# A graph-attention layer on one Trainium2 core: a branch mark for TensorE, a separate bank for a quarter of an accumulator, and a reordered last stage without GpSimd

## The chip, the core and the metric

The kernel runs on one core of one Trainium2 chip. The core has five engines with an instruction queue each: TensorE (PE in the profile, with its weight loads as PEld), VectorE (DVE), ScalarE (ACT), GpSimd (POOL) and SyncE (SP), which issues most DMA transfers. Sixteen DMA engines serve all DMA queues of the core. Results of matmuls go to PSUM, which this kernel uses as eight banks of 128 partitions by 512 float32.

The metric is the device time of one execution in microseconds. The profile's span is shorter than that time, since it reaches only from the program's first to its last instruction.

## The reference

Two graph-attention layers, a residual and a layer norm, on 512 nodes of width 768. The edge list has 16,896 entries sorted by destination (8192 pairs in both directions and one loop per node).

```python
def gat_layer(x, W, a_s, a_d, b, edge_index, concat):
    h = (x @ W).reshape(n, H, C)
    alpha_s = jnp.einsum('nhc,hc->nh', h, a_s)
    alpha_d = jnp.einsum('nhc,hc->nh', h, a_d)
    e = jax.nn.leaky_relu(alpha_s[src] + alpha_d[dst], NEG_SLOPE)
    m = jax.ops.segment_max(e, dst, num_segments=n)
    e = jnp.exp(e - m[dst])
    denom = jax.ops.segment_sum(e, dst, num_segments=n)
    alpha = e / (denom[dst] + EPS)
    msg = h[src] * alpha[:, :, None]
    out = jax.ops.segment_sum(msg, dst, num_segments=n)
    return out.reshape(n, H * C) + b

h = jax.nn.elu(gat_layer(x, W1, a_src1, a_dst1, b1, edge_index, True))   # 8 heads of 768
out = gat_layer(h, W2, a_src2, a_dst2, b2, edge_index, True)             # 1 head of 768
return _layernorm(x + out, axis=-1)
```

## The kernel before, in words

The edge list is turned once into a dense 512 x 512 table of edge counts, so attention becomes dense matrix work. For each of the eight heads the kernel projects x, computes the logits, takes the masked softmax, multiplies the attention matrix with the projected features, applies elu and multiplies by that head's rows of W2, adding into `h2`. All products are made by fast matrix-multiplication schemes: seven products of half-size blocks P1 to P7 instead of eight, or fifteen of thirds, with sums of blocks on the vector engine before and after.

The order of instructions is written by hand. Strings such as `HEAD`, `SECOND`, `NEXT` and `END` list short names, and `run` calls the function behind each name in that order; each engine's queue is in the order in which its instructions were so emitted. The framework adds the semaphore waits. `mm` is a list of free PSUM banks: `mm.next()` takes the one that was freed longest ago, `mm.release` puts one back. A bank taken out and written by one engine is guarded as a whole against the others.

The **branch.** The first pass assumes a balanced edge list. It computes a flag, and after it `tc.If(again != 0, label="again")` (line 33) runs a general pass if the assumption failed. With these inputs it does not fail, so each engine's branch jumps over the whole general pass to the few closing instructions. `mark_branch_hint_location` marks that branch as likely taken for the engines it lists: ScalarE, VectorE and SyncE before the change.

The **last stage** (`END`, from `root` on) multiplies the attention matrix of layer 2 with `h2` by seven products for two row halves i = 0 and 1 (`final`, line 1348), which gives the four row tiles of the output: tiles 0 and 1 in the upper half, 2 and 3 in the lower. Three accumulators of 384 columns are used for each i:

- `A`, i: P1 and P2, the left half of tile i (`residual`, names `sA`, adds the residual x + b2 scaled by the softmax denominator).
- `B`, i: a copy of A after P1 (`fork`), then P6, P7 and P4: the left half of tile 2 + i. After P6 and after P7 the vector engine reads it (`zu`, `zw`).
- `F`, i: starts from the residual (`seed`), then P5. `y22` (line 1400 or 1402) reads it for the right half of tile 2 + i, which goes to the output buffer `y`. `sF` (`less_first`, line 1387) adds another residual in place, and P3 completes the right half of tile i. For i = 1, P3 is made in two column quarters `f.P3.1a` and `f.P3.1b` (`final_part`, line 1371).

The softmax denominator is not divided out; the layer norm's epsilon is scaled instead. For each tile t follow statistics of its halves (`bn`, lines 1412 and 1415), their aggregate and the square root on ScalarE (`all`, lines 1433 and 1435), the reciprocal and the offset on VectorE (`inv`, lines 1440 and 1442), and the scaling with the store: `whole` for tiles 0, 2 and 3 (line 1450 on GpSimd for the right half of tile 3, line 1448 on ScalarE for the rest; one store of 384 KB by SyncE, line 1462), `left1` and `right1` for tile 1, the last (VectorE with SyncE's store, ScalarE with its own store, 192 KB each, line 1455). After the branch, SyncE waits for every store's semaphore (line 33), and the launch's closing barrier (line 1514) ends the program.

Of the kernel before, what the change touches and what calls it, by code (L numbers as in the profile page):

```python
# [13 lines left out]
AF = mybir.ActivationFunctionType  # L14
ALU = mybir.AluOpType
# [22 lines left out]
def gat_pass(  # L38
# [29 lines left out]
    L, R = slice(0, HALF), slice(HALF, D)  # L68
# [38 lines left out]
    mm, held = Ring(banks[:3]), Ring(banks[3:])  # L107
# [197 lines left out]
    general = flag is None  # L305
# [10 lines left out]
    else:  # L316
# [5 lines left out]
        for c in range(EC):  # L322
            m = (c + 0.5) * P * N / E
# [34 lines left out]
        for j in range(2):  # L358
            for r in range(2):
# [10 lines left out]
                                op0=ALU.mult, op1=ALU.add)  # L370
# [45 lines left out]
    HS, AL, BC = {}, {}, {}  # L416
# [307 lines left out]
    def run(script, ops):  # L724
        for name in script.split():
            ops.pop(name)()

    def softmax(q, h):
        ops = {}

        def token(t):
            def up():
                q[t] = lift(h, t)

            def out():
# [27 lines left out]
    again = None  # L763
    if not general:
# [72 lines left out]
        ops = {f"hot{j}": f for j, f in enumerate(f for q_ in range(NT) for f in one_hots(q_))}  # L837
# [15 lines left out]
    else:  # L853
        for t in range(NT):
            ps = mm.next()
            for c in range(EC):
# [3 lines left out]
                                        op0=ALU.is_equal)  # L860
# [245 lines left out]
    ops = softmax(q, 0)  # L1106
# [13 lines left out]
    mm = Free([banks[(mm.at + 1 + j) % 3] for j in range(3)] + banks[3:])  # L1120
# [18 lines left out]
    def hold():  # L1139
# [25 lines left out]
        P61 P70 u1 w0 x0 w.P6 P71 P40 b0 vadd ls2 P30 w.P10 q.P1 q.P4 q.P7 y0 ld1 w1 B0 P51 P62 P41 u2 x1 w.P2 b1 P72 w2 ls3  # L1165
        ld2 P31 P42 f0 y1 B1 P52 f1 F0 m.P2 x2 b2 F1 g.P9 P32 B2 g.P12 y2 m.P9 e.P2 f2 m.P12 ld3 F2 g.P7 rows0 e.P9 g.P1 w.P3
        rows1 row2 e.P12 g.P13 m.P1 g.P6 g.P11 spread e.P1 m.P0 own m.P13 2lift1 2lift2 2lift0 2leak1 g.P10 e.P0 2rank1 e.P13
        2lift3 2leak0 2rank0 m.P10 m.P4 2part1 e.P10 2leak2 2part0 g.P8 m.P11 e.P4 2rank2 2leak3 m.P6 seed g.P3 m.P8 g.P14
        e.P6 2den0 2den2 2part2 2in1 m.P14 2rank3 e.P11 e.P8 g.P5 e.P14 2den3 2part3 m.P3 2in2 m.P7 2in0 2den1 e.P3 m.P5 e.P7
        2in3 root c0 a0 f.P1.0 f.P1.1 e.P5 seed0 seed1 f.fork0 a1 c1 f.P5.0 sA0 f.P6.0 a2 c2 f.P2.0 zu0  # L1170
        f.fork1 f.P7.0 a3 c3 f.P6.1 zw0 f.P4.0 y22.0 sq2 sF0 f.P3.0 zu1 bn2L sA1 all2 f.P7.1 bn0L bn0R inv2 whole2 all0 f.P5.1
        zw1 f.P4.1 inv0 whole0 y22.1 sF1 f.P2.1 bn3R bn3L all3 f.P3.1a bn1L inv3 f.P3.1b whole3 bn1Ra bn1Rb all1 hint inv1 left1
        right1"""
    NEXT = ["""t.P11 e.P3.1 T.P6 t.P1 M.P8 T.P2 t.P13 E.P8 T.P4 M.P13 E.P13 in1 M.P9 l0 E.P9 l1 in2 M.P2 E.P2 M.P4 T.P10 T.P0 E.P4
        in3 M.P12 E.P12 l2 T.P1 M.P6 r0 M.P0 E.P6 E.P0 M.P1 r1 E.P1 M.P10 r2 E.P10 M.P5 r3 E.P5 M.P14 T.P7 E.P14 l3 M.P11
        T.P3 E.P11 src2 M.P7 M.P3 E.P7 E.P3 dst3 dst2 src3""",
# [16 lines left out]
    for h in range(H - 1):  # L1193
        last = h + 2 == H
        ops = mixed(h, AA, BB)
# [44 lines left out]
        else:  # L1240
            G, gsums = g_thirds()
# [4 lines left out]
        if h == 0 and not general:  # L1246
            again = nc.values_load(flag[:1, :1], min_val=0, max_val=E)
# [19 lines left out]
    xr = load_x()  # L1267
# [59 lines left out]
    ops.update({f"2den{t}": dens_(t) for t in range(NT)})  # L1327
# [12 lines left out]
    bank, stats, mv, rstd, off = {}, {}, {}, {}, {}  # L1340
# [18 lines left out]
    def seed_(i):  # L1359
        def f():  # L1360
            bank["F", i] = mm.next()
            nc.scalar.activation(bank["F", i][:, :HALF], xr[:, 2 + i, L], AF.Copy, scale=whole_den[2 + i])
        return f

    Q = HALF // 2
    quarters = (slice(0, Q), slice(Q, HALF))

    def final_part(j):
        def f():
            for k in range(2):  # L1370
                nc.tensor.matmul(bank["F", 1][:, quarters[j]], A2["P3"][:, k, P:2 * P], C2["P3"][:, k, quarters[j]],
                                 start=False, stop=k == 1, skip_group_check=True)
        return f

    def part(name, i):
        return bank[name, i][:, :HALF]
# [6 lines left out]
        return lambda: nc.vector.scalar_tensor_tensor(part("A", i), xr[:, i, L], whole_den[i], part("A", i), op0=ALU.mult,  # L1383
                                                      op1=ALU.add)

    def less_first(i):
        return lambda: nc.vector.tensor_tensor(part("F", i), part("F", i), xr[:, i, R], op=ALU.add)
# [4 lines left out]
    y = [None]  # L1392

    def lower_right(i):
        def f():
            if y[0] is None:
                y[0] = hpool.tile([P, NT, D], F32, name="hs")
            o = y[0][:, 2 + i, R]
            if i:
                nc.vector.tensor_tensor(o, part("F", i), xr[:, 2 + i, R], op=ALU.add)  # L1400
            else:
                nc.vector.scalar_tensor_tensor(o, part("F", i), 1.0, xr[:, 2 + i, R], op0=ALU.mult, op1=ALU.add,
                                               accum_out=total)
        return f

    def half_of(t, cols):
        if cols == R:
            return part("F", t) if t < 2 else y[0][:, t, R]
        return part("A", t) if t < 2 else part("B", t - 2)

    def moments(t, cols):
        return lambda: nc.vector.bn_stats(stats[t][:, 0 if cols == L else 1, :], half_of(t, cols))

    def moments_part(j):
        return lambda: nc.vector.bn_stats(stats[1][:, 1 + j, :], part("F", 1)[:, quarters[j]])

    def spread_of(t):

# [23 lines left out]
            nc.vector.scalar_tensor_tensor(off[t], mv[t][:, 0:1], -1.0, rstd[t], op0=ALU.mult, op1=ALU.mult)  # L1442
        return f

    def scale(t, cols, engine):
        o = y[0][:, t, cols]
        if engine == nc.scalar:
            nc.scalar.activation(o, half_of(t, cols), AF.Identity, bias=off[t], scale=rstd[t])
        else:
            engine.tensor_scalar(o, half_of(t, cols), mv[t][:, 0:1], rstd[t], op0=ALU.subtract, op1=ALU.mult)  # L1450

    def row_out_half(cols, engine, queue):
        def f():
            scale(1, cols, engine)
            queue.dma_start(out[P:2 * P, cols], y[0][:, 1, cols])
        return f

    def row_out_whole(t):
        def f():
            scale(t, L, nc.scalar)  # L1460
            scale(t, R, nc.gpsimd if t == 3 else nc.scalar)
            nc.sync.dma_start(out[t * P:(t + 1) * P, :], y[0][:, t, :])
        return f

    for i in range(2):
        for p, name in (("P1", "A"), ("P2", "A"), ("P6", "B"), ("P7", "B"), ("P4", "B"), ("P5", "F"), ("P3", "F")):
            if (p, i) != ("P3", 1):
                ops[f"f.{p}.{i}"] = final(p, i, name)
        ops.update({f"f.fork{i}": fork_(i), f"zu{i}": less_(i, i), f"zw{i}": less_(i, 2 + i), f"sA{i}": residual(i),
                    f"seed{i}": seed_(i), f"sF{i}": less_first(i), f"y22.{i}": lower_right(i)})  # L1470
# [11 lines left out]
    ops.update(left1=row_out_half(L, nc.vector, nc.sync), right1=row_out_half(R, nc.scalar, nc.scalar))  # L1482

    def hint():
        if not general:
            tc.mark_branch_hint_location("again", "LikelyTaken", [mybir.EngineType.Activation, mybir.EngineType.DVE, mybir.EngineType.SP])
    ops["hint"] = hint
    run(END, ops)
    return again

# [28 lines left out]
```

## Time and profile before

| what | value |
|---|---|
| time, median of 3 runs (lowest to highest) | 612.53 us (611.76 to 612.70) |
| the profiled execution's own time | 611.53 us |
| its span, first to last instruction | 609.7 us |
| granted TensorE clock, mean | 0.997 |
| TensorE matmuls, busy | 600.4 us (98% of the span) |
| VectorE, busy | 517.9 us (85%) |
| ScalarE, busy | 305.4 us (50%) |
| GpSimd, busy | 100.6 us (17%) |

Busy time counts arithmetic and weight loads, not waits, branches, semaphores or the issuing of DMA transfers; these stand in the trace under the engine's name with a q behind it. A timeline row gives start and length in microseconds, engine, source line, operation, written tile, read tiles, shape and count, and in brackets how long the engine had been idle and what released it. `hs`, `mm`, `tr`, `bc`, `st` are the program's names of tiles: `mm`, `tr` and `bc` are the PSUM banks, `hs` is here the residual or the output buffer.

### The profile page before, as it was taken

The numbers are of one execution on the slowest core, as the hardware profiler recorded it, in microseconds if no ns is written. First come the engines' busy times: TensorE is split into PE (matmuls) and PEld (weight loads), VectorE is DVE, ScalarE is ACT, GpSimd is POOL, SyncE is SP. The second block draws the span as 40 slices with busy tenths as digits, with TensorE's granted clock in tenths as the row PEclk, the third lists the DMA queues.
The fourth block names the chain that finished last, engine by engine and source line by source line (L and its number), as shares of the span: only waits on it lengthen the run. The fifth ranks groups of instructions, "written<-read, shape, count | busy, mean of one in ns | idle before, by whom it ended". The sixth has DMA issues, their size and how long they took to land.

```text
span 609.7 us, 8353 instructions
## 1 busy us (share of the span) xinstructions
PE 600.4 (98%) x2812; PEld 492.3 (81%) x2812; DVE 517.9 (85%) x1027; ACT 305.4 (50%) x563; POOL 100.6 (17%) x140
## 2 busy tenths in 40 slices
PE   9999999999999999999999999999999999999994
PEld 5665685788888888888888888888888888887863
DVE  7979968779997789878897789977897789989984
ACT  3128776624745166442746066532755147744743
POOL 2210103040301302022300303012210304022001
PEclk9999999999999999999999999999999999999998
DMA  8973898794947959395955939297883949593203
GB/s 302 314 169 90 251 273 200 217 287 78 346 70 237 212 179 244 51 336 81 330 110 174 268 127 291 47 300 133 273 167 113 294 92 261 104 238 56 53 17 109
DMA packets 97343, 114.24 MB, mean 187 GB/s; under 512 B 42966, under 2 KB 78222, under 8 KB 96398
## 3 DMA queue, kind: packets, MB, share of 16 engines
q1 hardware_dynamic: 75230, 89.26, 45.9%
q0 software_dynamic: 21632, 23.79, 24.6%
q10 hardware_dynamic: 432, 0.59, 0.3%
q8 instruction: 24, 0.39, 0.3%
q14 instruction: 25, 0.20, 0.1%
HBM read 99.05 MB, written 2.90 MB: 167 GB/s over the span
## 4 chain that ended last, share of the span: by engine, by line
PE 98%; DVE 0%; ACT 0%; issue 0%; DVEq 0%
PE mm L552 22%; PE mm L472 18%; PE mm L986 17%; PE mm L413 12%; PE tr L552 5%; PE bc L986 4%; PE tr L472 4%; PE bc L472 4%; PE tr L986 3%; PE bc L552 3%; PE mm L1348 2%; PE mm L663 1%; PE bc L792 1%; PE tr L413 1%; PE bc L271 1%; PE bc L1348 0%
## 5 line engine op out<-in xcount | busy, mean ns | idle before, releaser
L560 DVE TENSOR_TENSOR h<-h,mm 128x512 f32<-128x512 f32 x74 | 50.5, 683 | 8.9 <-PE mm L552 8.1
L478 ACT ACTIVATE hs<-mm 128x512 f32<-128x512 f32 x26 | 15.5, 597 | 80.6 <-PE mm L472 79.9
L187 POOL DMA_DIRECT2D w2t<-in_L_gnn_W_dram x21 | 28.3, 1662 | 165.9 <-PE mm L472 84.0
L480 DVE TENSOR_TENSOR hs<-hs,mm 128x512 f32<-128x512 f32 x38 | 26.1, 687 | 27.0 <-PE mm L472 19.9
L986 PE MATMUL mm<-PT,hs 128*128 128x256 f32 x192 | 46.6, 380 | 0.0
L552 PE MATMUL mm<-w1r,gT 128*128 128x256 f32 x192 | 44.2, 380 | 0.0
L915 ACT ACTIVATE q<-q,rden 128x512 f32<-128x512 f32 x28 | 20.2, 720 | 42.7 <-DVE rden L899 42.5
L923 ACT COPY PT<-zr 128x1024 uint16<-128x1024 uint16 x35 | 40.4, 1158 | 2.2 <-DMA zr<-pS 1.2
L187 POOL DMA_DIRECT2D w2r<-in_L_gnn_W_dram x14 | 18.3, 1310 | 139.4 <-DVE gT L1038 77.3
L552 PEld LDWEIGHTS mm<-w1r,gT 128*128 128x128 f32 x192 | 36.4, 190 | 5.2 <-DVE gT L589 0.3
L986 PEld LDWEIGHTS mm<-PT,hs 128*128 128x128 f32 x192 | 36.2, 190 | 5.2 <-ACT u L997 0.2
L703 ACT ACTIVATE q<-q,nmax 128x512 f32<-128x512 f32 x36 | 26.0, 722 | 25.9 <-DVE nmax L700 25.9
L472 PE MATMUL mm<-w2r,gT 128*128 128x256 f32 x144 | 33.7, 379 | 0.0
L422 DVE SCALAR_TENSOR_TENSOR scr<-hs,a_s 128x768 bf16<-128x768 f32 x32 | 30.6, 955 | 0.7
L422 DVE SCALAR_TENSOR_TENSOR scr<-hs,a_d 128x768 bf16<-128x768 f32 x32 | 30.5, 952 | 0.3
L472 PEld LDWEIGHTS mm<-w2r,gT 128*128 128x128 f32 x144 | 27.3, 190 | 3.8 <-issue 0.2
L552 PE MATMUL mm<-w1t,gS 128*128 128x256 f32 x128 | 30.2, 379 | 0.0
L472 PE MATMUL mm<-w2r,xT 128*128 128x256 f32 x128 | 29.9, 379 | 0.0
L986 PE MATMUL mm<-pS,gS 128*128 128x256 f32 x120 | 29.3, 379 | 0.0
L918 ACT COPY pS<-q 128x1024 uint16<-128x1024 uint16 x27 | 28.1, 1045 | 0.7
L472 PEld LDWEIGHTS mm<-w2r,xT 128*128 128x128 f32 x128 | 24.3, 190 | 3.3
L552 PEld LDWEIGHTS mm<-w1t,gS 128*128 128x128 f32 x128 | 24.3, 190 | 3.3
(393 smaller groups left out, 1493.2 us busy)
## 6 DMA issues: line engine op xcount, KB each, us to landing
w2r<-in_L_gnn_W_dram SPq DMA_DIRECT2D x48, 384.0 KB
w1r<-in_L_gnn_W_dram SPq DMA_DIRECT2D x43, 384.0 KB
gT<-xd SPq DMA_DIRECT2D x6, 1280.0 KB
w2t<-in_L_gnn_W_dram SPq DMA_DIRECT2D x21, 256.0 KB
w2t<-in_L_gnn_W_dram POOLq DMA_DIRECT2D x21, 256.0 KB, 9.3
w1t<-in_L_gnn_W_dram SPq DMA_DIRECT2D x18, 256.0 KB
w1t<-in_L_gnn_W_dram POOLq DMA_DIRECT2D x18, 256.0 KB, 5.1
w2r<-in_L_gnn_W_dram POOLq DMA_DIRECT2D x14, 256.0 KB, 8.7
```

Of the source, the lines that this page charges most:

```text
L187: return lambda: nc.gpsimd.dma_start(o, part(k, n), accum_op=add)
L413: nc.tensor.matmul(ps[:, :HALF], A_[p][:, k, i * P:(i + 1) * P], B_[p][:, k, :], start=start and k == 0, stop=k == HK - 1, skip_group_chec ...
L422: return [lambda al=al, a=a, sign=sign: nc.vector.scalar_tensor_tensor(scr, HS[h][:, t, :], sign, a, op0=ALU.mult, op1=ALU.mult, accum_out ...
L472: nc.tensor.matmul(bank[chain][:, i * TH:(i + 1) * TH], A_[p][:, k, i * P:(i + 1) * P], B_[p][:, k, :], start=first and i == k == 0, stop= ...
L480: nc.vector.tensor_tensor(out(o), out(o), ps, op=how)
L552: nc.tensor.matmul(bank[chain][:, i * TH:(i + 1) * TH], A_[p][:, k, i * P:(i + 1) * P], B_[p][:, k, :], start=first and i == k == 0, stop= ...
L560: nc.vector.tensor_tensor(out(o), out(o), ps, op=how)
L703: nc.scalar.activation(q, q, AF.Exp, bias=nmax, scale=-1.0, accum_out=dens[t])
L915: nc.scalar.activation(q, q, AF.Copy, scale=rden)
L918: nc.scalar.copy(apart.rearrange("p (h n) -> p h n", h=2), q.bitcast(U16).rearrange("p (n h) -> p h n", h=2))
L923: copy(PT.rearrange("p s n -> p (s n)").bitcast(U16).rearrange("p (s n h) -> p s n h", s=NT, h=2)[:, :, t * P:(t + 1) * P, :], parted.pop( ...
L986: nc.tensor.matmul(st[bank][:, :HN], A_[p][:, k, c * P:(c + 1) * P], B_[p][:, k, :], start=start and k == 0, stop=k == 1, skip_group_check ...
```

## The change

Four edits, all in the last stage or for it.

1. `hintT` in `END`: the branch is marked as likely taken for TensorE too.
2. The bank that held the broadcast logits row of layer 2 (`BC[H]`) is put back into the list of free banks once its last reader has been emitted (`freed`). From it, indirectly, comes one more bank `G`: the add `sF1` is split in two column quarters, `sF1a` writes its sum to `G`, `sF1b` works in place in F, 1. `f.P3.1a`, its statistics `bn1Ra` and its scaling use `G`. The scaling of tile 1's right half becomes two instructions of 192 columns on ScalarE, followed by one store as before.
3. Both halves of tile 3 are scaled by ScalarE; GpSimd has no instruction left in the last stage.
4. The order: `y22.1` stands ahead of `inv0`, and the right statistics, left statistics and aggregate of tile 3 (`bn3R bn3L all3`) stand ahead of `sF1a`, with `inv3` and `whole3` between `sF1a` and `sF1b`. The order of the matmuls is the same.

```diff
-        2lift3 2leak0 2rank0 ...
+        2lift3 freed 2leak0 2rank0 ...
...
-        f.fork1 f.P7.0 a3 c3 f.P6.1 zw0 f.P4.0 y22.0 sq2 sF0 f.P3.0 zu1 bn2L sA1 all2 f.P7.1 bn0L bn0R inv2 whole2 all0 f.P5.1
-        zw1 f.P4.1 inv0 whole0 y22.1 sF1 f.P2.1 bn3R bn3L all3 f.P3.1a bn1L inv3 f.P3.1b whole3 bn1Ra bn1Rb all1 hint inv1 left1
-        right1"""
+        f.fork1 f.P7.0 a3 c3 f.P6.1 zw0 f.P4.0 y22.0 sq2 sF0 f.P3.0 zu1 bn2L sA1 all2 hintT f.P7.1 bn0L bn0R inv2 whole2 all0 f.P5.1
+        zw1 f.P4.1 y22.1 inv0 whole0 bn3R bn3L all3 f.P2.1 sF1a inv3 whole3 sF1b f.P3.1a f.P3.1b bn1L bn1Ra bn1Rb all1 hint inv1
+        left1 right1"""
...
+    ops.update(..., freed=lambda: mm.release(BC[H]))
...
     def final_part(j):
...
-                nc.tensor.matmul(bank["F", 1][:, quarters[j]], A2["P3"][:, k, P:2 * P], C2["P3"][:, k, quarters[j]],
+                nc.tensor.matmul(bank[("F", 1) if j else "G"][:, quarters[j]], A2["P3"][:, k, P:2 * P], C2["P3"][:, k, quarters[j]],
...
-    def less_first(i):
-        return lambda: nc.vector.tensor_tensor(part("F", i), part("F", i), xr[:, i, R], op=ALU.add)
+    def less_first(i, cols=slice(0, HALF)):
+        def f():
+            if cols == quarters[0]:
+                bank["G"] = mm.next()
+            nc.vector.tensor_tensor(bank["G" if cols == quarters[0] else ("F", i)][:, cols], bank["F", i][:, cols],
+                                    xr[:, i, HALF + cols.start:HALF + cols.stop], op=ALU.add)
+        return f
...
     def row_out_whole(t):
         def f():
-            scale(t, L, nc.scalar)
-            scale(t, R, nc.gpsimd if t == 3 else nc.scalar)
+            for cols in (L, R):
+                by_scalar(t, y[0][:, t, cols], half_of(t, cols))
             nc.sync.dma_start(out[t * P:(t + 1) * P, :], y[0][:, t, :])
         return f
+
+    def last_left():
+        by_vector(1, y[0][:, 1, L], half_of(1, L))
+        nc.sync.dma_start(out[P:2 * P, L], y[0][:, 1, L])
+
+    def last_right():
+        for j in range(2):
+            o = y[0][:, 1, HALF + j * Q:HALF + (j + 1) * Q]
+            by_scalar(1, o, bank[("F", 1) if j else "G"][:, quarters[j]])
+        nc.scalar.dma_start(out[P:2 * P, R], y[0][:, 1, R])
...
+    def hint_tensor():
+        if not general:
+            tc.mark_branch_hint_location("again", "LikelyTaken", [mybir.EngineType.PE])
+    ops["hintT"] = hint_tensor
```

`by_scalar` is one activation (Identity with scale and bias), `by_vector` one subtract and multiply; both replace the former `scale`.

More of the change, by code (lines that the diff above doesn't have):

```diff
@@ L1167, in gat_pass @@
         rows1 row2 e.P12 g.P13 m.P1 g.P6 g.P11 spread e.P1 m.P0 own m.P13 2lift1 2lift2 2lift0 2leak1 g.P10 e.P0 2rank1 e.P13
-        2lift3 2leak0 2rank0 m.P10 m.P4 2part1 e.P10 2leak2 2part0 g.P8 m.P11 e.P4 2rank2 2leak3 m.P6 seed g.P3 m.P8 g.P14
+        2lift3 freed 2leak0 2rank0 m.P10 m.P4 2part1 e.P10 2leak2 2part0 g.P8 m.P11 e.P4 2rank2 2leak3 m.P6 seed g.P3 m.P8 g.P14
         e.P6 2den0 2den2 2part2 2in1 m.P14 2rank3 e.P11 e.P8 g.P5 e.P14 2den3 2part3 m.P3 2in2 m.P7 2in0 2den1 e.P3 m.P5 e.P7
         2in3 root c0 a0 f.P1.0 f.P1.1 e.P5 seed0 seed1 f.fork0 a1 c1 f.P5.0 sA0 f.P6.0 a2 c2 f.P2.0 zu0
-        f.fork1 f.P7.0 a3 c3 f.P6.1 zw0 f.P4.0 y22.0 sq2 sF0 f.P3.0 zu1 bn2L sA1 all2 f.P7.1 bn0L bn0R inv2 whole2 all0 f.P5.1
-        zw1 f.P4.1 inv0 whole0 y22.1 sF1 f.P2.1 bn3R bn3L all3 f.P3.1a bn1L inv3 f.P3.1b whole3 bn1Ra bn1Rb all1 hint inv1 left1
-        right1"""
+        f.fork1 f.P7.0 a3 c3 f.P6.1 zw0 f.P4.0 y22.0 sq2 sF0 f.P3.0 zu1 bn2L sA1 all2 hintT f.P7.1 bn0L bn0R inv2 whole2 all0 f.P5.1
+        zw1 f.P4.1 y22.1 inv0 whole0 bn3R bn3L all3 f.P2.1 sF1a inv3 whole3 sF1b f.P3.1a f.P3.1b bn1L bn1Ra bn1Rb all1 hint inv1
+        left1 right1"""
     NEXT = ["""t.P11 e.P3.1 T.P6 t.P1 M.P8 T.P2 t.P13 E.P8 T.P4 M.P13 E.P13 in1 M.P9 l0 E.P9 l1 in2 M.P2 E.P2 M.P4 T.P10 T.P0 E.P4
@@ L1326, in gat_pass @@
     ops.update({f"2{n}": f for n, f in softmax(q2, H).items()})
-    ops.update({f"2den{t}": dens_(t) for t in range(NT)})
+    ops.update({f"2den{t}": dens_(t) for t in range(NT)}, freed=lambda: mm.release(BC[H]))
     ts = nc.vector.tensor_tensor
@@ L1414, in moments_part @@
     def moments_part(j):
-        return lambda: nc.vector.bn_stats(stats[1][:, 1 + j, :], part("F", 1)[:, quarters[j]])
+        return lambda: nc.vector.bn_stats(stats[1][:, 1 + j, :], bank[("F", 1) if j else "G"][:, quarters[j]])
     def spread_of(t):
@@ L1443, in inverse, with by_scalar, by_vector @@
         return f
[L1445 to L1456, printed above, removed]
+    def by_scalar(t, o, p):
+        nc.scalar.activation(o, p, AF.Identity, bias=off[t], scale=rstd[t])
+    def by_vector(t, o, p):
+        nc.vector.tensor_scalar(o, p, mv[t][:, 0:1], rstd[t], op0=ALU.subtract, op1=ALU.mult)
     def row_out_whole(t):
         def f():
-            scale(t, L, nc.scalar)
-            scale(t, R, nc.gpsimd if t == 3 else nc.scalar)
+            for cols in (L, R):
+                by_scalar(t, y[0][:, t, cols], half_of(t, cols))
             nc.sync.dma_start(out[t * P:(t + 1) * P, :], y[0][:, t, :])
         return f
+    def last_left():
[6 more added lines that the diff above has]
+        nc.scalar.dma_start(out[P:2 * P, R], y[0][:, 1, R])
     for i in range(2):
@@ L1469, in gat_pass @@
         ops.update({f"f.fork{i}": fork_(i), f"zu{i}": less_(i, i), f"zw{i}": less_(i, 2 + i), f"sA{i}": residual(i),
-                    f"seed{i}": seed_(i), f"sF{i}": less_first(i), f"y22.{i}": lower_right(i)})
+                    f"seed{i}": seed_(i), f"y22.{i}": lower_right(i)})
+    ops.update(sF0=less_first(0), sF1a=less_first(1, quarters[0]), sF1b=less_first(1, quarters[1]))
     ops.update({f"f.P3.1{c}": final_part(j) for j, c in enumerate("ab")})
@@ L1481, in gat_pass @@
             ops[f"whole{t}"] = row_out_whole(t)
-    ops.update(left1=row_out_half(L, nc.vector, nc.sync), right1=row_out_half(R, nc.scalar, nc.scalar))
+    ops.update(left1=last_left, right1=last_right)
     def hint():
```

## The prediction

> **What bounds the kernel now.** I read the page first, then the last 13 us in the timeline, then the queue instructions behind the last arithmetic, and last the DMA queues in narrow windows there. The page says that TensorE is the chain:
>
> ```profile
> span 609.7 us, 8353 instructions
> PE 98%; DVE 0%; ACT 0%; issue 0%; DVEq 0%
> ```
>
> The change adds, drops and reorders no matmul, so it can move only what follows TensorE's end at 601.7 us, and through waits that end itself. The timeline (start, length, engine, line; in brackets the idle time before):
>
> ```profile
> 586.06 2.74 PE L1348 MATMUL mm<-xT,pS 128*128 128x384 f32 x8
> 587.12 1.07 PEld L1348 LDWEIGHTS mm<-xT,pS 128*128 128x128 f32 x4 [0.22 <-DVE xT L1338]
> ...
> 596.38 1.45 PE L1348 MATMUL tr<-xT,pS 128*128 128x384 f32 x4
> ...
> 597.02 0.69 ACT L1448 ACTIVATE hs<-hs,off,rstd 128x384 f32<-128x384 f32 x1
> 597.62 0.28 ACT L1435 ACTIVATE rstd<-mv,eden 128x1 f32<-128x1 f32 x1
> 597.67 1.45 PE L1348 MATMUL mm<-xT,PT 128*128 128x384 f32 x4
> ...
> 597.93 0.16 DVE L1440 RECIPROCAL rstd<-rstd 128x1 f32<-128x1 f32 x1 [0.73 <-ACT rstd L1435]
> 598.13 0.16 DVE L1442 SCALAR_TENSOR_TENSOR off<-mv,rstd 128x1 f32<-128x1 f32 x1
> 598.21 0.55 DVE L1400 TENSOR_TENSOR hs<-tr,hs 128x384 f32<-128x384 f32 x1
> 598.32 1.23 ACT L1448 ACTIVATE hs<-mm,off,rstd 128x384 f32<-128x384 f32 x2 [0.43 <-DVE off L1442]
> ...
> 598.67 0.55 DVE L1387 TENSOR_TENSOR tr<-tr,hs 128x384 f32<-128x384 f32 x1
> ...
> 599.61 0.55 DVE L1412 BATCH_NORM_STATS2 st<-mm 128x6 f32<-128x384 f32 x1
> 599.93 1.49 PEld L1371 LDWEIGHTS tr<-h,pS 128*128 128x128 f32 x8
> 600.19 0.21 DVE L1433 BATCH_NORM_AGGREGATE mv<-st 128x2 f32<-128x12 f32 x1
> 600.25 1.46 PE L1371 MATMUL tr<-h,pS 128*128 128x192 f32 x8
> ...
> 601.29 1.65 POOL L1450 TENSOR_SCALAR hs<-hs,mv,rstd 128x384 f32<-128x384 f32 x1 [49.12 <-DVE off L1442]
> 601.37 0.67 ACT L1448 ACTIVATE hs<-mm,off,rstd 128x384 f32<-128x384 f32 x1 [0.65 <-DVE off L1442]
> 601.75 0.63 DVE L1415 BATCH_NORM_STATS2 st<-tr 128x6 f32<-128x192 f32 x2 [0.48 <-PE tr L1371]
> 602.42 0.24 DVE L1433 BATCH_NORM_AGGREGATE mv<-st 128x2 f32<-128x18 f32 x1
> 602.69 0.30 ACT L1435 ACTIVATE rstd<-mv,eden 128x1 f32<-128x1 f32 x1 [0.65 <-DVE mv L1433]
> ...
> 603.29 0.67 DVE L1450 TENSOR_SCALAR hs<-bc,mv,rstd 128x384 f32<-128x384 f32 x1
> 603.41 0.67 ACT L1448 ACTIVATE hs<-tr,off,rstd 128x384 f32<-128x384 f32 x1 [0.42 <-DVE off L1442]
> 603.99 0.33 SPq L1455 DMA_DIRECT2D out_dram<-hs  x1
> 604.11 0.36 ACTq L1455 DMA_DIRECT2D out_dram<-hs  x1
> ```
>
> The last arithmetic ends at 603.41 + 0.67 = 604.08, and the two halves of the last row tile are issued then. The span goes on for 5.6 us. The queue instructions say why (count, shortest/median/longest ns, first and last start):
>
> ```profile
> L33 PEldq COMPARE_BRANCH  x1: 3982/3982/3982, 599.3 to 599.3; - x1
> L33 DVEq COMPARE_BRANCH  x1: 89/89/89, 603.2 to 603.2; - x1
> L33 SPq COMPARE_BRANCH  x1: 73/73/73, 604.4 to 604.4; - x1
> L33 ACTq COMPARE_BRANCH  x1: 68/68/68, 604.5 to 604.5; - x1
> L33 SPq EVENT_SEMAPHORE  x8: 17/17/17, 604.9 to 607.9; - x8
> L1514 SPq EVENT_SEMAPHORE  x14: 17/28/28, 608.0 to 609.6; - x14
> L1514 ACTq BRANCH_PREFETCH_HINT  x1: 50/50/50, 0.7 to 0.7; - x1
> ```
>
> SyncE collects the landings; the last, of the half that ScalarE issued, comes at 607.9, 3.8 us after its issue, and from there the closing waits take a fixed 609.7 - 607.9 = 1.8 us. So **the end is set by the landing of the last half tile, not by an engine**. TensorE's unmarked branch costs 3.98 us, but it is over at 599.3 + 3.98 = 603.3, before the arithmetic is.
>
> Why the landing takes 3.8 us is seen in the DMA queues. Four windows, 604.0 to 604.2, 605.0 to 605.2, 606.05 to 606.2 and 607.05 to 607.6 (queue, packets, MB, share of 16 engines' time):
>
> ```profile
> q8 instruction: 1, 0.02, 39.9%
> ...
> q14 instruction: 2, 0.02, 19.8%
> ...
> q14 instruction: 2, 0.02, 25.8%
> ...
> q10 hardware_dynamic: 12, 0.01, 7.0%
> ```
>
> The queues named "instruction" load code. One 16 KB packet starts at 604.0 to 604.2 and holds its engine for 0.399 x 16 x 0.2 = 1.28 us; four of 8 KB start near 605.1 and 606.1, 0.198 x 16 x 0.2 / 2 = 0.32 us each. After 607.05 only 12 packets of the last half are left, 0.07 x 16 x 0.55 = 0.6 us of work, which is one engine at a time: the tail is a straggler behind the 16 KB block. I take that block for TensorE's: it follows its branch's end by 0.8 us, and it is the only size of this queue. The four small ones follow the branches of SyncE and ScalarE by 0.6 us, so I take two for theirs.
>
> **The change part by part.** *The freed bank* (`freed`) adds no instruction; later accumulators get a bank that was emptied earlier, and no wait for a bank shows on TensorE here: 0.
>
> *The mark for TensorE.* One instruction, 50 ns by the row of ScalarE's, at 0.7 us, before TensorE has work; were it issued in place, 0.05 us of its queue under 1.3 us of matmuls. It turns 3.98 us into about 0.08, at a place where 0.7 us of DVE and ScalarE work still cover it: 0 directly. What follows is that the next block is loaded near 600.2 instead of 604.1, beside row 0's output, which has 4 us to spare.
>
> *The order on DVE.* y22.1 now stands ahead of inv0. It waits for P5.1, which ends at 596.38 + 1.45 = 597.83, so it starts at 597.87; inv0's pair follows at 598.34 and 598.53, and ScalarE's two scales for row 0 start at 598.72 and not 598.32: row 0 is issued 0.40 late, which nothing waits for. Statistics of tile 3: the right at 598.60, the left when P4.1 is done (597.67 + 1.45 = 599.12), at 599.16 and not 599.61; its aggregate at 599.74 and not 600.19. Tile 3 is 0.45 ahead.
>
> *The quarters on DVE.* Then sF1a. A half-width statistics takes (0.63 for two) about 0.36, so I take 0.35 for the half-width add: 599.86 to 600.21. ScalarE's root waits behind row 0's second scale: 599.99 to 600.28; reciprocal and offset to 600.65; sF1b 600.57 to 600.92. Before, the whole add was done at 598.67 + 0.55 = 599.22 and TensorE loaded P3.1a's weights at 599.93. Now that load waits for sF1a: 600.26, 0.33 late. The row at 587.12 shows that a load after a 0.22 us wait left the eight matmuls at 586.06 unbroken, so loads have some slack: P3.1a starts between 600.3 and 600.5 (it was 600.25), P3.1b between 601.0 and 601.2 behind sF1b, TensorE ends 0.1 to 0.3 us later, near 601.85. **A new wait on TensorE.**
>
> *The bank of its own.* bn1Ra sat at 601.75 behind the last matmul of both quarters. It may now run at 601.3 while P3.1b computes; only bn1Rb is left behind the end: 601.88 instead of 602.04 (601.75 plus half of the pair's 0.63, less their overlap). The gain of 0.28 shrinks to 0.15 (0 to 0.28). Aggregate, root, reciprocal and offset keep their lengths: the left half ends at 603.81 and is issued at 603.84, 0.15 sooner.
>
> *The right half in two pieces on ScalarE.* Two full scales take 1.23, one 0.67, so they overlap by 0.11. The trace has no 192-wide one; the bounds are 0.30 (one element) and 0.67: a pair takes 0.49 to 1.23. I take the middle, 0.49 each, 0.87 for the pair, since width is halfway between the rows: 0.20 more than before. Against the 0.15 gained: issued at 604.16, 0.05 **later** than 604.11 (0.33 sooner to 0.56 later).
>
> *GpSimd out.* Row 3's right half took 1.65 on GpSimd from 601.29, so the row was issued at 602.95. Now ScalarE does both halves from 600.69 in about 1.24: 601.93, issued at 601.97, **1.0 us sooner**. ScalarE is free again long before its root at 602.5. The 384 KB are through near 603.8, before anything of the last tile, where they ended behind the 16 KB block.
>
> **The sum.** On the engine of the 16 KB block three things queued up: row 3's eight packets, the left's and the right's. With either the early row or the mark gone right, about 1 us leaves it, and it is no longer the last. What remains are the engines of the 8 KB blocks, which SyncE and ScalarE still load after their branches. There, 2 x 0.32 + 0.5 (the right half's eight packets, 0.6 x 8 / 12 = 0.4, rounded up) from 605.2 ends at 606.4 at best; at worst they end where the straggler's last stretch begins, 607.1. It ended at 607.5 (607.05 and 12 packets of the remaining 0.6 us, less the wait for the semaphore until 607.9). I take 606.8: **-0.7 us** (-0.3 to -1.1), with the 0.05 later issue inside it.
>
> The rule that speaks against the mark: the Trainium skill, page "Runtime: NRT & Kernel Launch", section "Instruction fetch mechanics", says that prefetch is purely sequential and that a taken branch out of the window must fetch before it goes on. The 3.98 us agree, the 68 to 89 ns of the three marked branches do not: marks work here. By the rule the mark would do nothing, and the sum would stand on the early row 3 alone.
>
> The profiled execution took 611.53 with its span of 609.7; the median shown is 612.53, 1.0 above it. I take the shift off the median: 612.53 - 0.7 = **611.8 us** (610.8 for a profiled execution like this one).
>
> **The rivals.** *A. The small blocks hold the end.* The 8 KB blocks, four of them, drag the last half to 607.1 or more and the right half is late: -0.1 to 0, 612.4. For: all four lie in the last stretch. Against: they carry half the time of the large one. *B. All clear.* If the small blocks belong partly to GpSimd, whose branch moves to an early time, the last half lands as soon as the bulk, near 606.0: -1.5, 611.0. For: GpSimd branches late as well now. Against: the 0.6 us between ScalarE's and SyncE's branches and the blocks. *C. Slower: the right half is late.* ScalarE's pair costs its upper bound, 0.56 more, TensorE's 0.3 at the quarters eats the bank's 0.28, and the landing follows the issue one to one while the small blocks leave nothing to win: 612.53 + 0.56 + 0.02 = 613.1. With the queues' 0.7 won it decides only once the right half is issued after 604.11 + 0.7 = 604.8. For: the two pieces are certain. Against: the middle price. *D. The mark does harm.* If TensorE's marked target were loaded in place of its next block, it would stall once in the stream, by the same 3.98 us: 616.5. Against: three engines carry such a mark and none shows it. *E. The mark does nothing*: the branch still takes 4 us; the time is that of the forecast, and I count it there.
>
> **How the numbers follow.** Forecast 0.55, A 0.20, B 0.13, C 0.09, D 0.03. I count as no change what is within 0.2% (1.2 us: under 611.3 is faster, over 613.8 slower), about what a measurement of this kernel can tell. Faster: most of B (0.10) and a fifth of the forecast (0.11), 0.21. Slower: D, and a little of C and of the runs' own spread (611.76 to 612.70): 0.06. No change: 0.73. Range: from B, 610.9, to C short of its end, 612.9.
>
> **What would show it.** Right: TensorE's branch under 0.1 us; no 16 KB code packet after 601; row 3 issued near 602.0; the right half's add in two, TensorE's end at 601.8 to 602.0; the right half issued at 604.1 to 604.2; last landing near 607.2. Wrong: the right half issued under 603.9 (the pair was cheap, TensorE did not wait) or over 604.5; a landing that stays at 607.9 with the 16 KB block gone.

## The result and the profile after

The changed kernel takes 610.84 us (median of 22 runs, 610.18 to 612.03), the kernel before 612.07 us beside it (22 runs, 610.92 to 613.08). The ratio is 0.998, with a 95% interval of 0.9974 to 0.9986: **1.2 us faster** (0.9 to 1.6). The forecast was 0.7 us, and the measured time lies 0.06 us below the range of the prediction.

The profiled execution took 611.07 us with a span of 609.3 us, only 0.4 us less span than before. The reason is at the other end. Two groups of TensorE's timeline in the first 9 us, of the kernel before:

```profile
5.47 0.42 PE L360 MATMUL tr<-ident,idx_f 66*128 66x66 f32 x4
5.72 2.80 PE L663 MATMUL mm<-w1r,xT 128*128 128x384 f32 x8
```

and of the changed one:

```profile
5.52 0.65 PE L360 MATMUL tr<-ident,idx_f 66*128 66x66 f32 x4
5.96 3.37 PE L663 MATMUL mm<-w1r,xT 128*128 128x384 f32 x8
```

In this execution TensorE fell 0.8 us behind between 5.5 and 6.4 us, in these two groups. From there to matmul 2805 of 2812, 594 us later, every matmul of the two traces stands at the same distance to within 0.1 us. In the other profiles below the distance to the kernel before likewise changes by less than 0.2 us between 25 us and the last stage. So what sets two profiles apart ahead of the last stage happens in the first 25 us, and **the last stage has to be compared from a point inside it**. I take the end of P4.1, the matmul group that ends in both kernels before any change of the order can reach TensorE, and call the time from there to the end of the span the stretch: before, 597.67 + 1.45 = 599.12 and 609.7, 10.53 us; after, 598.46 + 1.45 = 599.91 and 609.3, 9.37 us (with the trace's own digits). It shrank by 1.16 us, close to the measured gain.

The timeline after, from P4.1 on (line numbers have moved; L1390 is the add in quarters, L1451 ScalarE's scaling):

```profile
598.46 1.45 PE L1348 MATMUL mm<-xT,PT 128*128 128x384 f32 x4
...
598.66 0.56 DVE L1405 TENSOR_TENSOR hs<-mm,hs 128x384 f32<-128x384 f32 x1 [0.68 <-PE mm L1348]
...
599.95 0.57 DVE L1417 BATCH_NORM_STATS2 st<-mm 128x6 f32<-128x384 f32 x1
600.55 0.21 DVE L1438 BATCH_NORM_AGGREGATE mv<-st 128x2 f32<-128x12 f32 x1
600.67 0.34 DVE L1390 TENSOR_TENSOR mm<-mm,hs 128x192 f32<-128x192 f32 x1
...
601.07 1.36 PEld L1371 LDWEIGHTS mm<-h,pS 128*128 128x128 f32 x8 [0.48 <-DVE mm L1390]
601.07 1.66 PE L1371 MATMUL mm<-h,pS 128*128 128x192 f32 x8
...
601.39 0.36 DVE L1390 TENSOR_TENSOR mm<-mm,hs 128x192 f32<-128x192 f32 x1
...
602.13 0.35 DVE L1420 BATCH_NORM_STATS2 st<-mm 128x6 f32<-128x192 f32 x1
602.14 0.70 ACT L1451 ACTIVATE hs<-hs,off,rstd 128x384 f32<-128x384 f32 x1
602.76 0.37 DVE L1420 BATCH_NORM_STATS2 st<-mm 128x6 f32<-128x192 f32 x1 [0.28 <-PE mm L1371]
...
604.21 0.92 ACT L1451 ACTIVATE hs<-mm,off,rstd 128x192 f32<-128x192 f32 x2 [0.48 <-DVE off L1447]
604.74 0.33 SPq L1465 DMA_DIRECT2D out_dram<-hs  x1
605.16 0.36 ACTq L1471 DMA_DIRECT2D out_dram<-hs  x1
```

Counted from P4.1's end, the last half is issued at 5.25 us where it was 4.98: the arithmetic got 0.27 us **slower**. TensorE's quarters (601.07 and 1.66) end at 2.82 instead of 2.59, since the weight loads wait for the add (the wait for its first quarter costs 0.13 us, the one for its second 0.09); the second quarter's statistics start at 2.85 instead of 2.91, so the bank of its own brings 0.06; the right half in two pieces costs 0.92 instead of 0.67, and ScalarE starts it 0.10 us behind the offset instead of 0.04.

The whole gain, and more, lies behind the issue. The queue instructions of the line of the branch, after:

```profile
L33 SPq EVENT_SEMAPHORE  x8: 17/17/17, 605.7 to 607.6; - x8
L33 POOLq COMPARE_BRANCH  x1: 45/45/45, 550.5 to 550.5; - x1
L33 PEldq COMPARE_BRANCH  x1: 393/393/393, 601.8 to 601.8; - x1
```

The last landing is seen at 607.57, **2.41 us after the issue of the last half; it was 3.83** (607.94 and 604.11). The closing waits take 1.70 us as before. 0.27 - 1.42 - 0.01 = -1.16. TensorE's marked branch takes 0.39 us instead of 3.98, and GpSimd branches at 550.5 instead of 601.2. The DMA queues after, in the windows 602.8 to 603.0, 605.3 to 605.6 and 606.5 to 607.0:

```profile
q8 instruction: 1, 0.02, 36.0%
...
q14 instruction: 1, 0.01, 6.4%
...
q14 instruction: 2, 0.02, 9.6%
```

The 16 KB code packet starts at 602.9, before any packet of the last row tile. Of the small code packets of the last stores three are left instead of four, and two of these come when most of the last half has passed.

This 16 KB packet is not the late one of the kernel before at another place. That kernel has one behind the start of TensorE's branch too, at 600.3, in the window 600.2 to 600.4:

```profile
q8 instruction: 1, 0.02, 44.6%
```

In each trace of this case one such packet starts 1.0 to 2.0 us after the start of TensorE's branch. The kernels without the mark have a second one, 0.8 to 1.8 us after the end of the long branch, and only that one is gone with the mark.

### The profile page after: what moved, and what is told of

Read it like the earlier page. It is cut to its first block, busy times and chain, and to the rows that moved or that the text cites. A ratio compares the mean times of both kernels' runs of the same rounds, so it can differ in the third digit from the quotient of the medians.

```text
span 609.3 us, 8356 instructions
## 1 busy us (share of the span) xinstructions
PE 601.4 (99%) x2812; PEld 492.8 (81%) x2812; DVE 518.1 (85%) x1028; ACT 306.2 (50%) x565; POOL 98.9 (16%) x139
## 4 chain that ended last, share of the span: by engine, by line
PE 99%; DVE 0%; ACT 0%; issue 0%; DVEq 0%; ACTq 0%
PE mm L552 22%; PE mm L472 18%; PE mm L986 17%; PE mm L413 12%; PE tr L552 5%; PE bc L986 4%; PE tr L472 4%; PE bc L472 4%; PE tr L986 3%; PE bc L552 3%; PE mm L1348 2%; PE mm L663 1%; PE bc L792 1%; PE tr L1348 1%; PE tr L413 1%; PE bc L271 1%
```

## The experiments

All were timed in five rounds beside the kernel before. The stretch and the issue are from each run's one profile, from the end of P4.1; its end is known as above. Where two of these kernels are compared, a difference of some tenths between their stretches is no finding by itself: against the kernel before, the change of the stretch and that of the median differ by up to 0.5 us in most rows, and by 0.7 and 0.85 in two (row 3 late, quarters early).

| kernel | median us | before, beside it | ratio, 95% interval | stretch us | last half issued |
|---|---|---|---|---|---|
| before | 612.07 | | | 10.53 | 4.98 |
| changed | 610.84 | 612.07 | 0.9980 (0.9974 to 0.9986) | 9.37 | 5.25 |
| mark alone | 611.21 | 612.04 | 0.9984 (0.9975 to 0.9993) | 9.83 | 4.99 |
| GpSimd out alone | 612.07 | 612.04 | 0.9997 (0.9988 to 1.0006) | 10.42 | 4.98 |
| mark and GpSimd out | 610.66 | 612.04 | 0.9973 (0.9962 to 0.9984) | 9.43 | 4.98 |
| changed without the mark | 612.15 | 612.04 | 0.9999 (0.9990 to 1.0008) | 10.85 | 5.25 |
| changed, GpSimd branches late | 610.58 | 612.35 | 0.9972 (0.9962 to 0.9983) | 9.22 | 5.25 |
| changed, quarters of the add early | 610.67 | 612.35 | 0.9974 (0.9964 to 0.9984) | 9.70 | 5.17 |
| mark, GpSimd out, P3 whole | 610.91 | 612.35 | 0.9977 (0.9968 to 0.9987) | 9.57 | 4.88 |
| changed, TensorE branches late | 611.23 | 612.35 | 0.9981 (0.9972 to 0.9990) | 9.74 | 5.25 |
| mark, row 3 early, idle GpSimd | 611.02 | 611.93 | 0.9984 (0.9975 to 0.9993) | 9.35 | 4.98 |
| the same, ScalarE waiting for GpSimd | 611.92 | 611.97 | 0.9997 (0.9989 to 1.0006) | 10.57 | 5.86 |
| mark, row 3 late | 611.93 | 612.53 | 0.9992 (0.9983 to 1.0001) | 10.61 | 4.98 (left half 5.26) |
| mark, GpSimd out, P3 whole, SyncE stores | 610.84 | 611.97 | 0.9982 (0.9973 to 0.9990) | 9.51 | 5.14 |
| changed, SyncE stores | 610.79 | 611.97 | 0.9979 (0.9970 to 0.9989) | 9.71 | 5.25 |

**The mark alone.**

```diff
-    tc.mark_branch_hint_location("again", "LikelyTaken", [Activation, DVE, SP])
+    tc.mark_branch_hint_location("again", "LikelyTaken", [Activation, DVE, SP, PE])
```

> The kernel before with the branch marked for TensorE and nothing else. Block theory (code loaded by the DMA engines during the last stores sets the last landing): TensorE's 16 KB block leaves the last microseconds, the four 8 KB blocks stay; the last half, issued where it was, lands about 3.4 us after its issue instead of 3.8: -0.4 us, and the 16 KB packet stands near 600. Row theory (the early store of row tile 3 is what frees the end): no change, within 0.2 us. Mark theory (the mark alone is the gain): -1.2 us.

Measured: -0.8 us, stretch 9.83. The window 600.2 to 600.4 of its DMA queues and its line of the branch:

```profile
q8 instruction: 1, 0.02, 43.2%
...
L33 PEldq COMPARE_BRANCH  x1: 393/393/393, 599.2 to 599.2; - x1
```

The large packet at 600.3 is the only one left, and the last half lands 3.13 us after its issue, not 3.83. Between the block theory's price and the mark theory's.

**GpSimd out alone.**

```diff
-            scale(t, R, nc.gpsimd if t == 3 else nc.scalar)
+            scale(t, R, nc.scalar)
```

> The kernel before with both halves of row tile 3 scaled by ScalarE and nothing else: GpSimd's branch falls to about 552 us, row 3 is issued near 602.6 instead of 602.96, the issue of the last half stays. Block theory: GpSimd's 8 KB block leaves the last microseconds, the 16 KB block at 604 stays: -0.2 to -0.6 us. Row theory: most of the gain of the whole change, about -1 us. Mark theory: no change.

Measured: no change, 10.42. Row 3 was issued at 3.54 instead of 3.84, and of the four small packets one is gone, but the second large one is there, later still: it starts at 5.83 us and not at 4.96 (window 605.2 to 605.4, where it overlaps the left half's packets), and the last landing is nearly where it was, 8.72 instead of 8.81:

```profile
q1 hardware_dynamic: 47, 0.07, 96.0%
q8 instruction: 1, 0.02, 29.0%
```

The last packets of the three stores stand behind the large one, which ends at 6.76: row 3's last ends at 7.08, the left half's at 7.78, the right half's at 8.27. With the mark alone the same three end at 6.02, 7.16 and 7.66. The row theory falls in its plain form: the early store alone frees nothing.

**Mark and GpSimd out.** Both diffs above.

> The kernel before with the mark for TensorE and with both halves of row tile 3 on ScalarE; no bank of its own, no new order, the last right half in one instruction. Block theory: both blocks are gone and the last half is issued 0.27 us sooner (against TensorE's end) than in the changed kernel, so it lands 2.4 us after its issue: -1.4 us, about 0.25 us faster than the changed kernel. If the bank and the order are worth something: -0.9 us or less, slower than the changed kernel.

Measured: -1.4 us, 9.43, the block theory's number, but not by its way: the last half lands 2.75 us after its issue, not 2.4, so the sooner issue brought nothing against the changed kernel. By the medians two edits that are worth 0.8 and 0 alone are worth 1.4 together; the three intervals are wide enough for a plain sum, too. Against the changed kernel the difference of 0.18 us in the medians (and 0.07 the other way in the stretch) is no difference: the bank of its own, the quarters and the order are worth nothing that shows.

**The changed kernel without the mark.**

```diff
-        ... bn2L sA1 all2 hintT f.P7.1 bn0L bn0R inv2 whole2 all0 f.P5.1
+        ... bn2L sA1 all2 f.P7.1 bn0L bn0R inv2 whole2 all0 f.P5.1
```

> The changed kernel without the mark for TensorE. Its branch takes 4 us again, from about 601.8 to 605.8, and the following 16 KB block is loaded near 606.6, in the middle of the last half's packets. Block theory: the landing is 0.3 to 0.8 us later than in the changed kernel: -0.5 to -0.9 us against the kernel before. Row theory: as the changed kernel, -1.2 us. Mark theory: no gain left.

Measured: nothing left of the gain, stretch 10.85, longer than before. The line of the branch, and the window 607.1 to 607.3:

```profile
L33 SPq EVENT_SEMAPHORE  x8: 17/17/17, 606.1 to 609.5; - x8
L33 PEldq COMPARE_BRANCH  x1: 3422/3422/3422, 602.3 to 602.3; - x1
...
q8 instruction: 1, 0.02, 30.2%
q14 instruction: 2, 0.02, 23.0%
q10 hardware_dynamic: 13, 0.01, 15.8%
```

The waiting weight loads hold TensorE's branch back by 1.7 us (1.90 after P4.1, 0.17 before). The branch without a mark then ends at 605.7, and the large packet starts at 607.2, in the middle of the last half (13 of its packets run in this window), and holds its engine's share of it back: the last landing is at 609.5. The block theory named the place rightly and the price too low; the time is the one that the mark theory gave. The mark is worth 1.2 to 1.3 us here, all of the gain.

**TensorE's branch late, mark kept.** One matmul of one column that waits for tile 1's aggregate, into an accumulator that nobody reads any more.

```diff
+    nc.tensor.matmul(bank["A", 0][:1, :1], mv[1][:, 0:1], ones, start=True, stop=True)   # after all1
```

> The changed kernel with one matmul of one column on TensorE that waits for tile 1's aggregate, into an accumulator that is no longer read: TensorE's marked branch comes about 1.7 us later. Block theory: the branch stays short (0.4 us), but the following 16 KB block starts 4.4 to 4.8 us after P4.1, as before the change, and holds one DMA engine during the last stores: stretch 9.8 to 10.4, +0.4 to +1.0. Mark theory (the length of the branch is what counted): 9.37, no change.

```profile
L33 PEldq COMPARE_BRANCH  x1: 388/388/388, 603.0 to 603.0; - x1
...
q8 instruction: 1, 0.02, 33.6%
```

The branch is as short as in the changed kernel; the large packet (window 604.1 to 604.3) has followed it to 4.87 us, close to the 4.96 of the late one before the change. Stretch 9.74, 0.4 more than the changed kernel's and just under the block theory's 9.8 to 10.4. The time does not settle it: the median is 0.4 above that of the changed kernel, but so is, by 0.3, that of the kernel before beside it, and the ratios are 0.9981 and 0.9980. It is 0.3 to 0.65 above the three other kernels timed beside the same kernel before. So by the profile, and less surely by the time, the **place of the code packet** costs. That the **length of the branch** itself does not is seen in the kernel before, where the branch ends at 4.16 us and TensorE then stands until the closing barrier lets it go at 9.87. The packet costs less here than in the kernel before, where row 3's last packet ends at 7.39; here it is through at 4.91.

**GpSimd's branch late.** One column on GpSimd after the root of tile 3.

```diff
+    nc.gpsimd.tensor_scalar(small.tile([P, 1], F32), rstd[3], 1.0, None, op0=ALU.mult)   # between inv3 and whole3
```

> The changed kernel with one GpSimd instruction of one column after the root of tile 3, written to a tile that nobody reads: GpSimd's branch stands in the last 10 us again, row 3 is still scaled by ScalarE and issued early. The stretch from the end of P4.1 to the end of the span was 10.53 us before, 9.37 in the changed kernel, 9.83 with the mark alone, 9.43 with mark and GpSimd out. Block theory: GpSimd's 8 KB block comes back near VectorE's and holds a second DMA engine: 9.7 to 9.9, +0.4 us. Row theory: what counts is the early store, 9.37, no change.

Measured: 9.22, no cost; the median is the lowest of all, within the noise. Two more small packets are there, at 2.9 and at 5.2; the second stands beside VectorE's, before the last half's first packet. So GpSimd's packets, at this place, cost nothing.

**What the second edit does once the mark is there.** GpSimd scales idly at its old place and time while ScalarE does row 3. The first form read the half that ScalarE overwrites, so ScalarE waited for GpSimd, the last half was issued at 5.86, and the run tells nothing (611.92 us, stretch 10.57):

```diff
+    nc.gpsimd.tensor_scalar(gT[:, 0, :HALF], y[0][:, 3, R], mv[3][:, 0:1], rstd[3], ...)   # first form
+    nc.gpsimd.tensor_scalar(gT[:, 0, :HALF], y[0][:, 0, R], mv[3][:, 0:1], rstd[3], ...)   # second form
```

> Mark, and both halves of row tile 3 on ScalarE, and GpSimd still scales that right half at the old place, into a tile nobody reads, so no store waits for it. It tells apart why the mark alone leaves a stretch of 9.83 us (from the end of P4.1 to the end of the span) and mark with GpSimd out one of 9.43. Block theory: GpSimd's late branch and its 8 KB block near 6.0 cost it: 9.8. Row theory for this part: row 3's store, 0.3 us sooner, is what counts: 9.43.

> As the run before it with GpSimd's idle work, but GpSimd now reads the finished half of row tile 0, so ScalarE does not wait for it: mark, row 3 on ScalarE and issued 3.53 us after P4.1, GpSimd's branch late as before the change. Stretch from the end of P4.1 to the end of the span: 9.83 with the mark alone, 9.43 with mark and GpSimd out. Block theory: GpSimd's 8 KB block near 6.0 costs the 0.4: 9.8. Row theory for this part: row 3's store, 0.3 us sooner, is what counts: 9.43.

The second form has stretch 9.35, with GpSimd's branch where the mark alone had it and row 3 issued 0.31 sooner. By this one profile it is row 3 and not GpSimd's packet. The small packets suggest how (windows 604.8 to 605.1 of the mark alone, 605.2 to 605.45 of this one; each holds VectorE's and GpSimd's):

```profile
q14 instruction: 2, 0.02, 13.0%
...
q14 instruction: 2, 0.02, 22.6%
```

Counted from P4.1 they start at 5.93 and 6.02 with the mark alone, where row 3's last packet ends at 6.02, and at 5.39 and 5.51 here, where it ends at 5.50. I read it as code packets that queue behind a store and are then late for the next one; no run moved them alone. The time does not separate the two kernels: both ratios are 0.9984.

**Row 3 later still.** The mark, and an idle GpSimd instruction of 192 columns ahead of GpSimd's half.

```diff
+    nc.gpsimd.tensor_scalar(gT[:, 0, :Q], y[0][:, 0, HALF:HALF + Q], mv[3][:, 0:1], rstd[3], ...)   # before whole3
```

> The kernel before with the mark, and one idle GpSimd instruction of 192 columns ahead of GpSimd's scaling of row tile 3: row 3 is issued about 0.9 us later (4.7 after P4.1 instead of 3.84), the last halves as before. Row theory: the store of row 3 now runs into those of the last tile on every DMA engine, the stretch grows from 9.83 to 10.2 to 10.6 and most of the mark's gain is lost (time within 0.4 us of the kernel before). If row 3's store does not count: 9.83, -0.8 us.

Measured: stretch 10.61, ratio 0.9992. By the profile the mark's gain is gone; by the time -0.5 us is left, which the interval puts between -1.0 and +0.1. The issues of its timeline show that it did more than planned, since the left half's store had to queue behind row 3's in SyncE's queue, 0.4 late:

```profile
602.59 1.64 POOL L1450 TENSOR_SCALAR hs<-hs,mv,rstd 128x384 f32<-128x384 f32 x1
604.25 0.33 SPq L1466 DMA_DIRECT2D out_dram<-hs  x1
604.40 0.36 ACTq L1455 DMA_DIRECT2D out_dram<-hs  x1
604.68 0.69 SPq L1455 DMA_DIRECT2D out_dram<-hs  x1
```

And it is that left half which ends last: its last packet ends at 8.26 us, the right half's at 7.63. So the run does not show the row theory; a store that queued in SyncE's queue set the end.

**Sooner arithmetic.** The quarters right behind y22.1, so that TensorE does not wait; and P3 of tile 1 made whole.

```diff
-        zw1 f.P4.1 y22.1 inv0 whole0 bn3R bn3L all3 f.P2.1 sF1a inv3 whole3 sF1b f.P3.1a f.P3.1b
+        zw1 f.P4.1 y22.1 sF1a sF1b inv0 whole0 bn3R bn3L all3 f.P2.1 inv3 whole3 f.P3.1a f.P3.1b
...
-        f.P3.1a bn1L inv3 f.P3.1b whole3 bn1Ra bn1Rb      (in mark and GpSimd out)
+        f.P3.1 bn1L inv3 whole3 bn1R
```

> The changed kernel with both quarters of the add right behind y22.1, so TensorE need not wait for them: its end falls from 2.82 to 2.59 us after P4.1, the last right half is issued 0.15 to 0.25 sooner. If the landing follows the issue: stretch 9.15 to 9.25, -0.2 us against the changed kernel. If VectorE's and ScalarE's small blocks hold the landing: 9.37, no change.

> Mark and GpSimd out, and P3 of tile 1 made whole, with one statistics instruction of 384 columns and two records to aggregate: 0.63 becomes 0.55 and 0.24 becomes 0.20, so the last half is issued 0.1 us sooner than with quarters (4.88 after P4.1 instead of 4.98). If the landing follows the issue: stretch 9.33. If the small blocks hold it: 9.43.

The last half was issued 0.08 and 0.10 us sooner than in the kernels they come from, and the stretches are 0.3 and 0.1 longer. That is within what one profile tells (times -1.7 and -1.4 us against before), and it is no gain: in these two and the two that they come from, with the last half issued anywhere from 4.88 to 5.25, the last packet runs at 7.2 to 7.3 after P4.1.

**SyncE stores the last half.**

```diff
-        nc.scalar.dma_start(out[P:2 * P, R], y[0][:, 1, R])
+        nc.sync.dma_start(out[P:2 * P, R], y[0][:, 1, R])
```

> Mark, GpSimd out, P3 of tile 1 whole, and both stores of the last tile issued by SyncE instead of one by ScalarE. SyncE's stores show their first packets 0.8 us after the issue, ScalarE's 1.2 us; SyncE issues the right half about 0.2 us later than ScalarE did, since the left one takes its queue for 0.33. If the landing follows the first packets: 0.2 us sooner than the same kernel with ScalarE's store (stretch 9.57): 9.35. If SyncE's small block, which then comes 0.35 later, holds the landing: no gain.

> The changed kernel with the last right half stored by SyncE instead of ScalarE. SyncE's queue is free when the second piece is scaled, so the issue stays at 5.25 after P4.1 and the first packets come 0.4 us sooner: stretch 8.95 instead of 9.37, the fastest so far, if the landing follows the packets; 9.37 if the small blocks hold it.

Neither is faster than its pair (610.84 for 610.91, 610.79 for 610.84). In the changed kernel the sooner first packets did not come about. SyncE's second issue, right behind its first, took 0.82 us and not 0.33:

```profile
604.29 0.33 SPq L1465 DMA_DIRECT2D out_dram<-hs  x1
604.71 0.82 SPq L1471 DMA_DIRECT2D out_dram<-hs  x1
```

The right half's packets run from about 6.6 us after P4.1, where ScalarE's ran from 6.2. No version tried beats the changed kernel by more than the measurement tells.

## Why the prediction was wrong

*The base*: the forecast of 611.8 us was taken off a median of three runs, 612.53. Beside the changed kernel the same program took 612.07 (22 runs). So about half of what the forecast was off, 0.46 us, is the base; the other half is the size of the change, -0.7 for a measured -1.2, and this lies outside the -0.3 to -1.1 of the prediction too.

*What bounds the kernel*: right. The end is the landing of the last half, and nothing before the last stage moved.

*The mark*: right that it is hidden itself and that its effect lies in the code packets; the late-branch run shows that the large one follows TensorE's branch. Wrong that the packet at 604.1 would move to 600.2: the kernel before has one there already, and the mark takes the second away. The first stands at 602.9 after the change (602.1 by the clock of the kernel before) and not before 601, since the new waits hold TensorE's branch back by 1.7 us, which the prediction left out. The expected 0.08 us for the branch was 0.39.

*The order and the new wait on TensorE*: as forecast, TensorE ends 0.23 later (0.1 to 0.3). But VectorE's aggregate of tile 3 came at 600.55 - 599.91 = 0.64 after P4.1, where I had 0.62, and then everything behind it a little later, so that the bank's 0.15 was 0.06. The pair on ScalarE cost 0.25, not 0.20, and small delays ahead of it another 0.08. The last half was issued 0.27 later instead of 0.05.

*Row 3*: 0.88 sooner against P4.1 (2.96 instead of 3.84); 1.0 was forecast. Its last packet ended at 5.46 us, 0.8 later than the 603.8 of the forecast.

*The sum* is where it failed, at two sentences. The first, that "with either the early row or the mark gone right, about 1 us leaves" the engine of the 16 KB packet, is wrong: the early row without the mark was worth nothing in two runs, because the packet then stands later and still in the way. Rival E, the mark without effect, would not have had the forecast's time but that of the kernel before. The second is the size: I let the last packet run at 606.8 for an issue at 604.16, 2.64 us after it, because ScalarE's and SyncE's small code packets would be in the way from 605.2 on. It ran 1.91 us after the issue (3.39 before), sooner than the best case of the prediction's sum, 606.4, which is 2.24 after it. The pair near 605.1 that the prediction took for theirs was GpSimd's and VectorE's: one packet of it vanished with GpSimd's branch. ScalarE's and SyncE's are the pair near 606.1; in the changed kernel they come 1.3 to 1.4 us after their branches, not 0.6, and so almost behind the last half. (With P3 whole the two late packets stand at 6.85 and 6.91 after P4.1; where SyncE also stores both halves and ScalarE branches 1.1 us sooner, at 6.73 and, the other, at 5.45 or 5.69.) So the term on the queues was -0.75 and measured -1.48 by the last packet, and the term on the issue +0.05 and measured +0.27. That these packets make up the whole difference is not shown: ScalarE's and SyncE's moved only together with a store. And where the sum's other end, the straggler at 607.1, would give -0.4, the range has -0.3.

Rival B, "all clear", had the nearest size, -1.5, and its premise holds: some of the small packets belong to GpSimd. But the run in which GpSimd branches late again lost nothing, so its way to that size is not shown. A, C and D did not happen: the small packets did not hold the end at its old place, ScalarE's pair was near the middle price, and no branch mark cost TensorE a block.

What stays open: whether, and by which path, row 3's 0.3 us and GpSimd's absence matter beside the mark (both together 0.55 us by the medians of the mark alone and of mark and GpSimd out, whose intervals overlap), and what holds the last packet at 7.2 to 7.3 us when the half is issued sooner. The code packet at 5.2 to 5.7, VectorE's by elimination, is on the way in each of these kernels, but it was not moved alone.

## What to carry to other kernels

When the end of a kernel is a landing and not an instruction, look at what else the DMA engines carry in that time. Code is among it: here each engine's last branch was followed by a code packet of 8 or 16 KB, and the last packets of the stores stood behind the large one. An unmarked branch that is over long before the end can still delay the end in this way. Mark such branches, and look at where their packets fall; the arithmetic may even get slower. And two edits that clear the same queue need not be a sum: test them together and each alone.

## What the runs showed of the hardware

- The marks are issued at 0.7 to 0.8 us and still work 600 us later: TensorE's branch fell from 3.98 to 0.39 us. The mark saves a code packet: the page counts 23 of 16 KB for 24, and the one that is missing is the second behind the branch:

```profile
q8 instruction: 23, 0.38, 0.2%
```

- A branch can be held back by a wait on a weight load that has nothing to do with it: it stands 1.7 us later in the changed kernel (1.90 after P4.1 for 0.17), and at 0.04 where the quarters of the add are early and no load waits. Without the mark this delay put its second code packet in the middle of the last half.
- A weight load of TensorE that started 0.35 us late put the start of its matmul only 0.03 us behind its place: the load and the matmul both start at 601.07. But that matmul's record is 0.43 us long instead of 0.33, and the next one starts 0.13 late.
- Executions of one program differ by almost 2 us (610.18 to 612.03), and the matmuls of two traces that differ part in the first 25 us: after that the distance changes by less than 0.2 us until the last stage.
